# Splitting a layer norm into three pieces and joining two products in the third layer of a four-layer kernel

## The chip, the cores and the metric

One Trainium2 chip, one core. The metric is the device time of one execution in microseconds; the median of three runs is given. All tensors are float32.

## The reference, cut to what matters

Four layers work on `x` of shape (4, 128, 64, 64): four images, 128 channels, 4096 positions (tokens). Layer 0 is a state-space block between convolutions, layer 1 a 3x3 convolution, layer 2 a softmax attention with feed-forward and a mixture of experts, layer 3 a linear attention and a second mixture of experts. The change is about the norm before the attentions and about the linear attention:

```python
def _ln_t(v, eps=1e-5):
    m = jnp.mean(v, axis=-1, keepdims=True)
    s = jnp.var(v, axis=-1, keepdims=True)
    return (v - m) / jnp.sqrt(s + eps)
...
phi_q = jax.nn.elu(q) + 1.0
phi_k = jax.nn.elu(k) + 1.0
KV = jnp.einsum('blhd,blhm->bhdm', phi_k, v)
K_sum = phi_k.sum(axis=1)
Z = 1.0 / (jnp.einsum('blhd,bhd->blh', phi_q, K_sum) + EPS)
V_new = jnp.einsum('blhd,bhdm->blhm', phi_q, KV) * Z[..., None]
out = V_new.reshape(bs, seq, N_HEADS * HEAD_DIM) @ Wo + bo
...
t = t + _L3_attn_ref(_ln_t(t), ...)
```

There are 8 heads of 16 channels; `q`, `k` and `v` are affine images of the normed tokens. `Z` is one number per token and head, so it may be multiplied to `phi_q` instead of to the product with `KV`; and then `KV` (one 16x16 block per head, zero elsewhere) and `Wo` may be multiplied with each other once per image.

## The kernel before, in words

Channels lie on the 128 partitions, tokens along the free axis, in chunks of 512 columns (`CH`), eight to an image (`NCH`). [...]

The order of the work. The code is a Python program that is unrolled. A stage of a layer is a generator: `in_turn(n, *stages)` runs over rounds, and in round i it calls the stages from the last to the first, stage k on chunk i-k, with a `yield` after each. `run(*parts)` steps several generators in turn, one `yield` each (`in_turns`), and so fixes the order in which instructions are written. The tile framework then orders the instructions of each engine; an instruction that is ready may pass one that was written before it. Only the attention of the second layer, with its long score and exponential loops, has a fixed order for PE, DVE and POOL. A `psum.tile(..., tag="mm")` takes a bank from a pool of that tag (7 banks in the third layer, 8 in the second from the second image on, 4 for the first, 6 in the expert layers); the framework takes care that it is free.

The norm, `layernorm_steps` (from line 102). A product with `center` takes the mean off the chunk (`ln_xc`, L94); ACT squares it and copies it to `ln_kept` (L115, L116), and a `yield` follows. Four products with `mean` put the variances of 128 tokens each into 32 rows of `ln_var` (L94); DVE transposes 32x32 blocks (L122); the inverse root of 4 numbers per partition is made either by POOL's `pow` (L142, behind an addition of eps on DVE, L141; the third layer) or by a square root on ACT and a reciprocal on DVE (L127, L128; the second layer); four PE transposes of the broadcast root spread it over the channels, into the same PSUM tile `ln_var` (L131), and DVE multiplies it to `ln_kept` (L133; with gain and bias L135, L136).

Callers. In the second layer three places use it: `centred`/`norm` of `prepare` (32 chunks), `first_centred`/`first_norm` and `last_centred`/`last_norm` of `feed_forward` (32 chunks each), 96 norms in all. A first call runs to the `yield`, a second one, a stage later, runs the rest. `prepare` of image b+1 and `feed_forward` of image b run side by side between two attentions; the first `prepare` runs beside the end of the first two layers, the last `feed_forward` alone. In the third layer, `K.layernorm` runs the whole norm in one stage.

The third layer, `layer3_attention`. `summed(b)` has the stages `norm`, `keys` and `add` in `in_turn`: `keys` multiplies the normed chunk with the keys' and values' weights (`kv`), adds the bias (L2068), copies values (L2074) and makes the feature elu+1 (L2076 and L2045); `add` sums features times values into `kv_sum`, 129 columns wide, the last for the sum of the features. At its end `kvh` (the masked KV) and `ksh` (the masked K_sum) are made. `answered(b)` has the stages `queries` (q and its feature `e_q`), `weighed` (`den_ps` from `ksh`, `num_ps` from `kvh`; DVE transposes `den`, adds, inverts, transposes back to `z`, L2118 to L2123, and multiplies `z` with `num_ps` to `vn`, L2125) and `give` (product with `wo`, added to the image, L2131). `summed(0)` runs alone, then `summed(b+1)` beside `answered(b)`, then `answered(3)` alone.

The expert layers (`expert_ffn`) have a norm of their own, in which the spread goes into a tile of its own, `ln_rs` (L1865); the change doesn't touch them.

Of the kernel before, what the change touches and what calls it, by code (L numbers as in the profile page):

```python
# [9 lines left out]
F32 = mybir.dt.float32  # L10
# [3 lines left out]
ALU = mybir.AluOpType  # L14
# [3 lines left out]
P = 128  # L18
# [3 lines left out]
CH = 512  # L22
NCH = L // CH
# [7 lines left out]
class Common:  # L31
# [61 lines left out]
    def mm(self, out, lhsT, rhs, start=True, stop=True):  # L93
        self.nc.tensor.matmul(out, lhsT, rhs, start=start, stop=stop)  # L94
# [7 lines left out]
    def layernorm_steps(self, out, terms, work, psum, affine=None, bufs=2, more=None, power=False):  # L102

        nc = self.nc
        xc = psum.tile([P, CH], F32, name="ln_xc", tag="mm")
        for n, (lhsT, rhs) in enumerate(terms):
            self.mm(xc, lhsT, rhs, start=n == 0, stop=n == len(terms) - 1)
        shift, g, b = affine or (0.0, None, None)
        sq = work.tile([P, CH], F32, name="ln_sq", bufs=bufs)
        kept = work.tile([P, CH], F32, name="ln_kept", bufs=bufs)  # L110
        if more is not None:
            nc.vector.scalar_tensor_tensor(kept, xc, shift, more, ALU.add, ALU.add)
            nc.scalar.activation(sq, kept, AF.Square)
        else:
            nc.scalar.activation(sq, xc, AF.Square, bias=shift)  # L115
            nc.scalar.activation(kept, xc, AF.Identity, bias=shift)  # L116
        yield
        vp = psum.tile([P, CH], F32, name="ln_var", tag="mm")
        for k in range(4):
            self.mm(vp[32 * k : 32 * k + 32, 0:P], self.mean[:, 0:32], sq[:, P * k : P * k + P])  # L120
        vt = work.tile([P, 4, 32], F32, name="ln_vt")
        nc.vector.transpose(vt.rearrange("p a b -> p (a b)"), vp[:, 0:P])  # L122
        sd = work.tile([P, 4], F32, name="ln_sd")
        if power:
            self.inverse_root(sd, vt[:, :, 0])()
        else:
            nc.scalar.activation(sd.unsqueeze(2), vt[:, :, 0:1], AF.Sqrt, bias=self.eps5)  # L127
            nc.vector.reciprocal(sd, sd)  # L128
        by_block = vp.rearrange("p (g b i) -> p b g i", b=4, i=32)
        for k in range(4):  # L130
            nc.tensor.transpose(by_block[:, k], sd[:, k : k + 1].to_broadcast([P, P]), self.ident)  # L131
        if affine is None:
            nc.vector.tensor_tensor(out, kept, vp, ALU.mult)  # L133
        else:
            nc.vector.scalar_tensor_tensor(kept, kept, g, vp, ALU.mult, ALU.mult)  # L135
            nc.gpsimd.tensor_scalar(out, kept, b, None, ALU.add)  # L136

    def inverse_root(self, out, src):
# [966 lines left out]
def in_turn(n, *stages):  # L1105


    for i in range(n + len(stages) - 1):
        for k in reversed(range(len(stages))):
            if 0 <= i - k < n:  # L1110
                stages[k](i - k)
                yield


def in_turns(*parts):

    parts = list(parts)
    while parts:
        for p in list(parts):
            try:  # L1120
                next(p)
            except StopIteration:
                parts.remove(p)
                continue
            yield
# [13 lines left out]
def layer2_attention(K, xd, dpool, w, before, images):  # L1139

    nc, tc, mm = K.nc, K.tc, K.mm
# [4 lines left out]
    with ExitStack() as ctx:  # L1146
# [107 lines left out]
        def prepare(b, big, work, psum):  # L1254
# [3 lines left out]
            n = NTT * NH * (HD + 1)  # L1258
# [5 lines left out]
            heads, xs, nrms, laters, halves = {}, {}, {}, {}, {}  # L1264
# [8 lines left out]
                next(halves[c])  # L1273

            def norm(c):
                next(halves.pop(c), None)
                nc.sync.dma_start(out=nrm_d[b % 2][:, c * CH : (c + 1) * CH], in_=nrms[c])

            def products(c):
# [60 lines left out]
            stages = in_turn(NCH, fetch, centred, norm, products, running, store)  # L1340
# [258 lines left out]
        def feed_forward(b, dsum, work, psum, into=None):  # L1599
# [67 lines left out]
                next(halves[c])  # L1667

            def first_norm(c):
                next(halves.pop(c), None)  # L1670

            def cosines(c):
                zp = psum.tile([P, CH], F32, name="z_ps", tag="mm")
# [29 lines left out]
                next(lasts[c])  # L1703

            def last_norm(c):
                next(lasts.pop(c), None)
                o = sums.pop(c)
                x = loads[c]
                nc.gpsimd.tensor_tensor(x, x, o, ALU.add)
                if into is None:  # L1710
                    nc.sync.dma_start(out=xd[b][:, c * CH : (c + 1) * CH], in_=x)
# [300 lines left out]
def layer3_attention(K, xs, w):  # L2012
# [3 lines left out]
    with ExitStack() as ctx:  # L2016
# [32 lines left out]
        def summed(b):  # L2049

            nrm = big.tile([P, L], F32, name="nrm")
            kvp = pskv.tile([P, P + 1], F32, name="kv_sum")
            phis = {}

            def norm(c):
                cols = slice(c * CH, (c + 1) * CH)
                K.layernorm(nrm[:, cols], xs[b][:, cols], work, psum)

            def keys(c):

                k1 = work.tile([P, 4, P], F32, name="k1")
                v = vs[(b * NCH + c) % 3]
                for i in range(2):
                    kv = psum.tile([P, 2, 2 * P], F32, name="kv", tag="mm")
                    for j in range(2):
                        at = c * CH + (2 * i + j) * P
                        mm(kv[:, j, :], nrm[:, at : at + P], wkv)
# [12 lines left out]
            def add(c):  # L2080
                ph, v = phis.pop(c)
                for j in range(4):
                    t = 4 * c + j
                    mm(kvp, ph[:, j, :], v[:, j, :], start=t == 0, stop=t == NTT - 1)

            yield from in_turn(NCH, norm, keys, add)

            kss = work.tile([P, 1], F32, name="kss")
            nc.vector.tensor_copy(kss, kvp[:, P : P + 1])
            kvh = work.tile([P, P], F32, name="kvh")  # L2090
            nc.vector.scalar_tensor_tensor(kvh, bv, kss, kvp[:, 0:P], ALU.mult, ALU.add)
            nc.vector.tensor_tensor(kvh, kvh, K.same16, ALU.mult)
            ksh = work.tile([P, P], F32, name="ksh")
            nc.vector.tensor_scalar(ksh, K.same16, kss, None, ALU.mult)
            kept[b] = nrm, kvh, ksh

        def answered(b):
            nrm, kvh, ksh = kept.pop(b)
            phis, vns = {}, {}

            def queries(c):
                qp = psum.tile([P, CH], F32, name="q_ps", tag="mm")
                mm(qp, wq, nrm[:, c * CH : (c + 1) * CH])
                q1 = work.tile([P, CH], F32, name="q1")
                nc.scalar.activation(q1, qp, AF.Identity, bias=bq1)
                e = phis[c] = work.tile([P, CH], F32, name="e_q")
                nc.scalar.activation(e, qp, AF.Exp, bias=bq)
                feature(e, e, q1)

            def weighed(c):  # L2110

                ph = phis.pop(c)
                dp = psum.tile([P, CH], F32, name="den_ps", tag="mm")
                mm(dp, ksh, ph)
                np_ = psum.tile([P, CH], F32, name="num_ps", tag="mm")
                mm(np_, kvh, ph)
                dt = work.tile([P, CH // 32, 2, HD], F32, name="den_t")
                nc.vector.transpose(dt.rearrange("p a h d -> p (a h d)"), dp)  # L2118
                rd = work.tile([P, CH // 32, 2, 1], F32, name="rd")
                nc.vector.tensor_scalar(rd, dt[:, :, :, 0:1], 1e-5, None, ALU.add)  # L2120
                nc.vector.reciprocal(rd, rd)
                z = work.tile([P, CH // 32, 2, HD], F32, name="z")
                nc.vector.transpose(z, rd.to_broadcast([P, CH // 32, 2, HD]))  # L2123
                vn = vns[c] = work.tile([P, CH], F32, name="vn")
                nc.vector.tensor_tensor(vn, z.rearrange("p a h d -> p (a h d)"), np_, ALU.mult)  # L2125

            def give(c):
                op = psum.tile([P, CH], F32, name="o_ps", tag="mm")
                mm(op, wo, vns.pop(c))
                at = xs[b][:, c * CH : (c + 1) * CH]  # L2130
                nc.vector.scalar_tensor_tensor(at, op, bo, at, ALU.add, ALU.add)  # L2131

            return in_turn(NCH, queries, weighed, give)
# [85 lines left out]
```

## Time and profile before

| what | us |
|---|---|
| median of 3 runs | 9518.07 (9507.56 to 9523.9) |
| the profiled execution | 9513.52 |
| its span, first to last instruction | 9511.7 |
| PE busy in the span | 8601.4 (90%) |
| PE weight loads | 3291.5 (35%) |
| DVE busy | 7152.9 (75%) |
| ACT busy | 7275.5 (76%) |
| POOL busy | 4928.9 (52%) |
| mean granted TensorE clock | 0.934 of full |

How to read it: busy time is the union of an engine's instructions. PE is TensorE's matmuls, PEld its weight loads, which overlap the matmuls; a float32 product appears as two instructions of each. [...] work back to back is better read from start to start. "Idle before" in square brackets is the time in which the engine stood still before an instruction, with what ended it. L94 is the helper through which all products go, so they are told apart by their tiles. The attention of the second layer takes most of the span: four stretches of some 1290 us, in which PE and ACT are busy almost throughout.

### The profile page before, as it was taken

The numbers are of one execution on the slowest core, as the hardware profiler recorded it, in microseconds if no ns is written. First come the engines' busy times: TensorE is split into PE (matmuls) and PEld (weight loads), VectorE is DVE, ScalarE is ACT, GpSimd is POOL, SyncE is SP. The second block draws the span as 40 slices with busy tenths as digits, with TensorE's granted clock in tenths as the row PEclk, the third lists the DMA queues.
The fourth block names the chain that finished last, engine by engine and source line by source line (L and its number), as shares of the span: only waits on it lengthen the run. The fifth ranks groups of instructions, "written<-read, shape, count | busy, mean of one in ns | idle before, by whom it ended". The sixth has DMA issues, their size and how long they took to land.

```text
span 9511.7 us, 189086 instructions
## 1 busy us (share of the span) xinstructions
PE 8601.4 (90%) x74394; PEld 3291.5 (35%) x74394; DVE 7152.9 (75%) x7845; ACT 7275.5 (76%) x10493; POOL 4928.9 (52%) x3287
## 2 busy tenths in 40 slices
PE   5888888889879999979999979999979999998887
PEld 2222222234443333333333333333333333334444
DVE  2889898887858888868888867888876888863463
ACT  3766767654459999969999969999979999974232
POOL 1777687765535555545555545555555555542011
PEclk8888888889989999989999989999989999999998
DMA  4434435222221221141121132221132121132205
GB/s 121 118 86 115 103 87 121 66 67 82 84 72 40 40 40 40 30 120 37 39 39 39 38 100 51 40 40 40 40 85 58 40 40 40 40 100 66 70 10 169
DMA packets 580323, 631.22 MB, mean 66 GB/s; under 512 B 118816, under 2 KB 374888, under 8 KB 578536
## 3 DMA queue, kind: packets, MB, share of 16 engines
q1 hardware_dynamic: 579432, 619.12, 26.4%
q8 instruction: 586, 9.60, 0.4%
q14 instruction: 305, 2.50, 0.1%
HBM read 444.74 MB, written 106.97 MB: 58 GB/s over the span
## 4 chain that ended last, share of the span: by engine, by line
PE 60%; DVE 4%; POOL 2%; issue 2%; ACT 2%; DMA 2%; SPq 1%; DVEq 0%; POOLq 0%; ACTq 0%
PE ctx_ps L94 28%; PE acc_ps L94 14%; PE score L94 12%; PE ln_xc L94 1%; PE hid_ps L94 1%; DMA w<-in_L_ffn_weight 1%; PE kv L94 1%; PE ln_var L131 1%; POOL ln_sd L1856 1%; DVE ctx L1509 0%; SPq L1244 0%; PE pool L94 0%; DVE x L2009 0%; POOL q L1304 0%; ACT hid L1696 0%
## 5 line engine op out<-in xcount | busy, mean ns | idle before, releaser
L1575 ACT ACTIVATE ex<-score 128x1024 f32<-128x1024 f32 x5120 | 4927.2, 1039 | 220.7 <-PE score L94 134.6
L94 PE MATMUL ctx_ps<-ex,qt 128*32 128x512 f32 x20480 | 2734.0, 606 | 19.8 <-DVE ctx L1509 19.8
L1524 POOL TENSOR_TENSOR folded<-ex 128x1024 f32<-128x1024 f32 x512 | 1224.0, 2391 | 2102.6 <-ACT ex L1575 1837.4
L1581 DVE STREAM_TRANSPOSE turned<-ex 128x1024 f32<-128x1024 f32 x1536 | 1886.0, 1228 | 325.4 <-ACT ex L1575 325.1
L1557 DVE STREAM_TRANSPOSE turned<-ex 128x1024 f32<-128x1024 f32 x1532 | 1842.6, 1203 | 0.0
L94 PE MATMUL acc_ps<-turned,turned_v 128*32 128x256 f32 x24576 | 1769.3, 379 | 3.0 <-POOL qt L1262 2.3
L94 PE MATMUL score<-queries,keys 32*128 32x512 f32 x10240 | 1333.7, 497 | 39.1 <-POOL queries L1252 33.4
L937 DVE TENSOR_TENSOR_SCAN hs<-decay,carry,hs 128x512 f32<-128x512 f32 x1024 | 1242.6, 1265 | 104.7 <-ACT decay L933 92.6
L94 PEld LDWEIGHTS acc_ps<-turned,turned_v 128*32 128x32 f32 x24576 | 800.5, 110 | 1476.9 <-issue 1324.3
L941 POOL TENSOR_TENSOR hs<-hs,c_sb 128x1024 f32<-128x1024 f32 x512 | 1207.4, 2358 | 80.8 <-DMA c_sb<-c_d 40.8
L933 ACT ACTIVATE decay<-dt,a_neg 128x512 f32<-128x512 f32 x1024 | 692.7, 689 | 646.5 <-DVE hs L937 637.5
L94 PEld LDWEIGHTS score<-queries,keys 32*128 32x128 f32 x10240 | 512.4, 182 | 1133.3 <-ACT ex L1575 775.5
L1381 POOL TENSOR_TENSOR turned_v<-v,quarter 128x1024 f32<-128x1024 f32 x256 | 612.8, 2394 | 262.9 <-PE acc_ps L94 230.7
L1525 POOL TENSOR_TENSOR quarters<-folded 128x512 f32<-128x512 f32 x512 | 658.2, 1286 | 40.2
L94 PE MATMUL y_ps<-hs,pair 128*64 128x512 f32 x2048 | 642.7, 754 | 35.6 <-POOL hs L941 35.3
L926 DVE TENSOR_TENSOR hs<-dtx,b_ps 128x2048 f32<-128x2048 f32 x256 | 580.7, 2268 | 110.5 <-PE b_ps L94 47.7
L94 PEld LDWEIGHTS ctx_ps<-ex,qt 128*32 128x32 f32 x20480 | 406.1, 108 | 655.5 <-issue 599.4
L94 PE MATMUL b_ps<-dbc,state 32*64 32x512 f32 x1024 | 328.3, 722 | 181.3 <-DVE hs L926 181.1
L1575 ACT ACTIVATION_READ_ACCUMULATOR ex<-score 128x1 f32 x2048 | 439.8, 215 | 0.0
L940 POOL COPY carry<-hs 128x2 f32<-128x2 f32 x512 | 97.4, 190 | 641.9 <-DVE hs L937 605.7
L1509 DVE COPY ctx<-ctx_ps 128x512 f32<-128x512 f32 x256 | 176.9, 691 | 329.4 <-PE ctx_ps L94 325.5
L1566 DVE TENSOR_REDUCE dacc<-quarters 128x2 f32<-128x512 f32 x508 | 327.4, 644 | 0.0
(376 smaller groups left out, 8800.6 us busy)
## 6 DMA issues: line engine op xcount, KB each, us to landing
c_sb<-c_d SPq DMA_DIRECT2D x512, 128.0 KB
keys<-head_d SPq DMA_DIRECT2D x1024, 64.0 KB
queries<-head_d SPq DMA_DIRECT2D x1024, 64.0 KB
under<-image_d SPq DMA_DIRECT2D x192, 264.0 KB
dt<-dt SPq DMA_DIRECT2D x128, 256.0 KB
dtx<-dtx SPq DMA_DIRECT2D x128, 256.0 KB
v<-value_d SPq DMA_DIRECT2D x1024, 32.0 KB
w<-in_L_ffn_weight SPq DMA_DIRECT2D x32, 1024.0 KB
```

Of the source, the lines that this page charges most:

```text
L94: self.nc.tensor.matmul(out, lhsT, rhs, start=start, stop=stop)
L926: nc.vector.tensor_tensor(hs, dtx2, bb.unsqueeze(1).to_broadcast([P, NQ, CH]), ALU.mult)
L933: nc.scalar.activation(ex, dt2[:, q, :], AF.Exp, scale=a_neg[:, q, g : g + 1])
L937: nc.vector.tensor_tensor_scan(hs[:, q, :], decays[q - 2 * i], hs[:, q, :], carry[:, g, q : q + 1], ALU.mult, ALU.add)
L941: nc.gpsimd.tensor_tensor(hs[:, two, :], hs[:, two, :], cs.unsqueeze(1).to_broadcast([P, 2, CH]), ALU.mult)
L1381: nc.gpsimd.tensor_tensor(t, v.unsqueeze(2).to_broadcast([P, 4 * BT, 4, HD]), quarter.unsqueeze(1).to_broadcast([P, 4 * BT, 4, HD]), ALU.mult,
L1524: nc.gpsimd.tensor_tensor(hs, exs[:, :, 0], exs[:, :, 1], ALU.add)
L1525: nc.gpsimd.tensor_tensor(qs, hs[:, :, 0 : CH // 2], hs[:, :, CH // 2 :], ALU.add)
L1557: nc.vector.transpose(*upright)
L1566: nc.vector.tensor_reduce(at, qs, AX.X, ALU.add)
L1575: nc.scalar.activation(ex, sps[p], AF.Exp, scale=scale, accum_out=sums[:, t : t + 1] if summed else None)
L1581: nc.vector.transpose(*upright)
```

## The change

- `layernorm_steps` has a second `yield` behind the inverse root, and the spread goes into a new PSUM tile `ln_rs` (tag `mm`); `ln_var` is only 128 columns wide. `ln_kept` gets one buffer more, `ln_sd` four in place of two.
- In the second layer, the callers run the generator to its end, so there the two last pieces follow each other directly.
- In the third layer the norm is three stages: `centred`, `varied`, `norm`. A new `in_rounds` takes stages with their lags; in a round it calls `varied` of the chunk before, `add` of the third before, `keys` of the second before, `norm` of the chunk before and `centred` of its own, with a `yield` after each. `summed` so has five steps per chunk.
- At the end of `summed`, `kvh` is transposed and multiplied with `wo` to `kvo`.
- `weighed` leaves `num_ps` out and multiplies `z` to the features; `give` multiplies them with `kvo` in place of `wo`.

```diff
-        kept = work.tile([P, CH], F32, name="ln_kept", bufs=bufs)
+        kept = work.tile([P, CH], F32, name="ln_kept", bufs=bufs + 1)
...
-        vp = psum.tile([P, CH], F32, name="ln_var", tag="mm")
+        vp = psum.tile([P, P], F32, name="ln_var", tag="mm")
         for k in range(4):
-            self.mm(vp[32 * k : 32 * k + 32, 0:P], self.mean[:, 0:32], sq[:, P * k : P * k + P])
+            self.mm(vp[32 * k : 32 * k + 32], self.mean[:, 0:32], sq[:, P * k : P * k + P])
         vt = work.tile([P, 4, 32], F32, name="ln_vt")
-        nc.vector.transpose(vt.rearrange("p a b -> p (a b)"), vp[:, 0:P])
-        sd = work.tile([P, 4], F32, name="ln_sd")
+        nc.vector.transpose(vt.rearrange("p a b -> p (a b)"), vp)
+        sd = work.tile([P, 4], F32, name="ln_sd", bufs=4)
         if power:
             self.inverse_root(sd, vt[:, :, 0])()
         else:
             nc.scalar.activation(sd.unsqueeze(2), vt[:, :, 0:1], AF.Sqrt, bias=self.eps5)
             nc.vector.reciprocal(sd, sd)
-        by_block = vp.rearrange("p (g b i) -> p b g i", b=4, i=32)
+        yield
+        rp = psum.tile([P, CH], F32, name="ln_rs", tag="mm")
+        by_block = rp.rearrange("p (g b i) -> p b g i", b=4, i=32)
         for k in range(4):
             nc.tensor.transpose(by_block[:, k], sd[:, k : k + 1].to_broadcast([P, P]), self.ident)
         if affine is None:
-            nc.vector.tensor_tensor(out, kept, vp, ALU.mult)
+            nc.vector.tensor_tensor(out, kept, rp, ALU.mult)
         else:
-            nc.vector.scalar_tensor_tensor(kept, kept, g, vp, ALU.mult, ALU.mult)
+            nc.vector.scalar_tensor_tensor(kept, kept, g, rp, ALU.mult, ALU.mult)
...
+def in_rounds(n, *stages):
+    for i in range(n + max(lag for lag, _ in stages)):
+        for lag, stage in stages:
+            if 0 <= i - lag < n:
+                stage(i - lag)
+                yield
...
             def norm(c):
-                next(halves.pop(c), None)
+                for _ in halves.pop(c):
+                    pass
...
+            def centred(c):
+                cols = slice(c * CH, (c + 1) * CH)
+                halves[c] = K.layernorm_steps(
+                    nrm[:, cols], [(K.center, xs[b][:, cols])], work, psum, bufs=3, power=True
+                )
+                next(halves[c])
+
+            def varied(c):
+                next(halves[c])
+
             def norm(c):
-                cols = slice(c * CH, (c + 1) * CH)
-                K.layernorm(nrm[:, cols], xs[b][:, cols], work, psum)
+                next(halves.pop(c), None)
...
-            yield from in_turn(NCH, norm, keys, add)
+            yield from in_rounds(NCH, (1, varied), (3, add), (2, keys), (1, norm), (0, centred))
...
-            kept[b] = nrm, kvh, ksh
+            tp = psum.tile([P, P], F32, name="kv_t", tag="mm")
+            nc.tensor.transpose(tp, kvh, K.ident)
+            kvt = work.tile([P, P], F32, name="kvt")
+            nc.vector.tensor_copy(kvt, tp)
+            both = psum.tile([P, P], F32, name="kvo_ps", tag="mm")
+            mm(both, kvt, wo)
+            kvo = work.tile([P, P], F32, name="kvo")
+            nc.vector.tensor_copy(kvo, both)
+            kept[b] = nrm, kvo, ksh
...
-                np_ = psum.tile([P, CH], F32, name="num_ps", tag="mm")
-                mm(np_, kvh, ph)
...
-                nc.vector.tensor_tensor(vn, z.rearrange("p a h d -> p (a h d)"), np_, ALU.mult)
+                nc.vector.tensor_tensor(vn, z.rearrange("p a h d -> p (a h d)"), ph, ALU.mult)
...
-                mm(op, wo, vns.pop(c))
+                mm(op, kvo, vns.pop(c))
```

The drain shown for `norm` is made in the same way in `first_norm` and `last_norm` of the second layer.

More of the change, by code (lines that the diff above doesn't have):

```diff
@@ L1669, in first_norm @@
             def first_norm(c):
-                next(halves.pop(c), None)
+                for _ in halves.pop(c):
+                    pass
             def cosines(c):
@@ L1705, in last_norm @@
             def last_norm(c):
-                next(lasts.pop(c), None)
+                for _ in lasts.pop(c):
+                    pass
                 o = sums.pop(c)
@@ L2053, in summed @@
             phis = {}
+            halves = {}
+            def centred(c):
[6 more added lines that the diff above has]
+                next(halves[c])
             def norm(c):
-                cols = slice(c * CH, (c + 1) * CH)
-                K.layernorm(nrm[:, cols], xs[b][:, cols], work, psum)
+                next(halves.pop(c), None)
             def keys(c):
@@ L2094, in summed @@
             nc.vector.tensor_scalar(ksh, K.same16, kss, None, ALU.mult)
-            kept[b] = nrm, kvh, ksh
+            tp = psum.tile([P, P], F32, name="kv_t", tag="mm")
[7 more added lines that the diff above has]
+            kept[b] = nrm, kvo, ksh
         def answered(b):
-            nrm, kvh, ksh = kept.pop(b)
+            nrm, kvo, ksh = kept.pop(b)
             phis, vns = {}, {}
```

## The prediction

> **What bounds the kernel now.** I began with the page's 40 slices: between the four attention stretches and at the end lie short stages that the long ones hide. The rows of the tiles that the diff names gave their places, and one table of stretches their size. Its columns are length, busy time of PE, PE's weight loads, DVE, ACT, POOL, then TensorE's granted clock.
>
> ```profile
> 4057.00:4243.00 186.00, 134.07 (x608) 63.31 (x608) 108.36 (x232) 119.70 (x182) 92.89 (x108) 0.79 0.51 131
> 8487.00:8604.00 117.00, 98.89 (x437) 43.07 (x437) 49.25 (x107) 74.28 (x113) 56.35 (x44) 0.88 0.56 168
> 8872.00:8946.00 74.00, 49.32 (x250) 31.97 (x250) 23.33 (x55) 21.20 (x43) 8.06 (x8) 0.86 0.00 1
> 8946.00:9181.00 235.00, 203.10 (x908) 115.18 (x903) 157.18 (x327) 88.19 (x166) 24.16 (x24) 1.00 0.00 1
> 9181.00:9226.00 45.00, 32.21 (x66) 11.70 (x65) 32.70 (x56) 10.14 (x16) 0.00 (x0) 0.95 0.07 24
> ```
>
> The last three rows are the third layer: `summed(0)` alone, three joint blocks of 78.9 us (first key product to first key product: 8949.94, 9028.82, 9107.70), and `answered(3)` alone: 354 us. The first two rows are second-layer stages that call the same edited norm: preparing one image beside the feed-forward of another (three like this, 180 to 186 us), and the last feed-forward alone. The chain that ended last names PE in nearly every step of the joint blocks. One round on PE:
>
> ```profile
> 8972.37 1.02 PE L94 MATMUL ln_xc<-x,center 128*128 128x512 f32 x2
> 8973.23 0.83 PE L94 MATMUL kv_sum<-v,e_k 128*128 128x129 f32 x6
> 8974.08 0.43 PE L94 MATMUL ln_var<-ln_sq,mean 128*32 128x128 f32 x8
> 8974.43 1.13 PE L94 MATMUL q_ps<-nrm,wq 128*128 128x512 f32 x2
> 8975.40 0.39 PE L94 MATMUL kv_sum<-v,e_k 128*128 128x129 f32 x2
> 8975.62 1.02 PE L94 MATMUL o_ps<-vn,wo 128*128 128x512 f32 x2
> 8976.76 0.65 PE L131 MATMUL ln_var<-ident,ln_sd 128*128 128x128 f32 x4
> 8978.26 0.48 PE L94 MATMUL kv<-wkv,nrm 128*128 128x256 f32 x1 [0.85 <-DVE nrm L133]
> ```
>
> Start to start, a 512-column product costs 0.86 us. A round is 9.44 us: five such products (den, num, centring, q, o) 4.30, keys and values 1.72, kv_sum 0.86, means 0.35, spreading transposes 0.44, together 7.67; the other 1.8 us waits for the norm, inverse root first, then L133.
>
> These lines also show how the order is made. `q_ps` needs nothing of this round and its bank is free, yet six kv_sum instructions, later in the program, pass it; it runs straight behind `ln_var`, the tile asked for before it. So I read: a product that opens a new PSUM tile does not pass an older one of the same tag, while one that writes an open tile can be passed. L131 (into `ln_var`, already open) is passed by q and o. The expert layer has the other kind, a spread into a tile of its own:
>
> ```profile
> 8606.80 1.12 PE L94 MATMUL ln_xc<-x,center 128*128 128x512 f32 x2
> 8610.16 0.66 PE L1865 MATMUL ln_rs<-ident,ln_wide 128*128 128x128 f32 x4 [2.24 <-POOL ln_wide L1858]
> 8610.75 1.08 PE L94 MATMUL ln_var<-ln_sq,mean 128*32 128x128 f32 x16
> 8611.76 1.22 PE L94 MATMUL ln_xc<-x,center 128*128 128x512 f32 x1
> ```
>
> PE idles 2.24 us, though the next centring needs only x, there all along, and the next means' squares ended at 8608.56. Now a second-layer round:
>
> ```profile
> 8593.41 0.42 PE L94 MATMUL ln_var<-ln_sq,mean 128*32 128x128 f32 x8
> 8593.76 1.13 PE L94 MATMUL ln_xc<-x,center 128*128 128x512 f32 x2
> 8594.72 1.88 PE L94 MATMUL ln_xc<-hid,w2T 128*128 128x512 f32 x4
> 8597.86 0.65 PE L131 MATMUL ln_var<-ident,ln_sd 128*128 128x128 f32 x4 [1.26 <-DVE ln_sd L128]
> 8598.35 1.02 PE L94 MATMUL ln_xc<-hid,w2T 128*128 128x512 f32 x2
> ```
>
> From means to spread 4.0 us pass (a table load of 1.28, square root 0.30, reciprocal 0.18, handoffs); the next chunk's centring and part of its product fill 2.7 of them.
>
> **The change, part by part.** *Product with values gone* (`num_ps`): PE loses 0.86 us a chunk. In the 24 joint rounds that is on the path. In `answered(3)` it is not: there o waits for vn on DVE, 1.24 us in a 4.94 us round, with four products (3.44 us) on PE. `vn` reads features from SBUF where it read PSUM: e_q, both operands in SBUF, takes 686 ns, vn 687, so nothing.
>
> *Norm in three pieces, alone* (`summed(0)`): PE's work is 7.67-4x0.86=4.23 us a chunk, DVE's 2.70 (k 2x0.425, e_k 0.682, transpose 0.312, eps 0.170, L133 0.688). Now 7.82 us a warm round, 73 us in all. Means still follow their square closely (Square 0.60), though kv_sum can fill that; I take 4.8 a round, eight rounds 38, plus about 11 of fill (first chain to the first key product 6.25 today, one more round behind): 49, so -24. Bounds -15 and -28.
>
> *Joint blocks.* Without num PE has 6.8 us a chunk; DVE has 2.70 and for the answer 4.09 (e_q 0.686, den_t 0.717, two small 0.536, z 0.712, vn 0.687, x 0.750): 6.8 as well. But steps alternate one for one, and `summed` now has 40 steps against 24 in `answered` (24 and 24 before). So the answers end when 60% of the sums is done: DVE 8x4.09+0.6x21.6=45.7 us there, PE 40.9; behind it 40% of the sums alone, PE 13.5. Floor 59. `answered(3)` keeps DVE 83% busy (4.09 of 4.94): the first part 55, the tail 3.2 rounds of 5.0, 16; 71 against 78.9, so -8 a block, -24. Bounds -51 (blocks of 62) and 0.
>
> *Joined matrix*, once an image: a transpose, two 128x128 copies (nearest: the mask of kvh, 0.285 each), a product of 0.22, handoffs: about 1.7 us. It is needed only at `give(0)`, behind queries and den, so it lies beside them; I take +2 for four images, bounds 0 and +7. Extra buffers for `ln_kept` and `ln_sd` issue nothing.
>
> Third layer: -24-24+2 = -46 (bounds -75 and -13).
>
> *The second layer is edited too.* All callers use the same generator, and they run its rest in one go, so the order of tiles becomes mean, spread, next product. The spread now opens `ln_rs`, so by the reading above, z, centring, hid, rd and den products queue behind a spread that waits for its root, and ACT, DVE and POOL wait for them. Work is unchanged; cover is lost. In the last feed-forward (16 norms, means to spread 3.6 us on average, 8.1 us of it idle today) up to 48 us of products lose their place. Serially: PE's 99 plus 16x3 for the roots (about the shortest of today, once queues have drained), its other waits (12) taken to overlap: 147 against 117, +30; bounds +10 and +48. In a mixed stage 24 norms have 6.3 us between means and spread, PE idles 52 us, 32 of it for the root. Serially 134+24x3=206, +20; with the 20 us of other waits kept, 226, +40. I take +35, bounds +5 and +70. Three of them +105. The first preparation runs beside the convolution, whose products have another tag: +2. Second layer: +137 (bounds +25 and +260).
>
> Two rules of the Trainium skill bear on this. "Perfetto Trace Analysis", section "Optimization Strategy", says that consistent bubbles can mean that SBUF or PSUM doesn't suffice for the next tile. By it, a mean tile given back at its transpose, instead of after L133, helps or costs nothing: sum -46. The 2.24 us row speaks against it: of six banks at most four were in use. I go by the row. "TensorE: Matmul & The Clock Gate", section "Part 1: The HAM clock gate", halves the clock after an idle window of about 3.4 us: gaps of 3 us lie near it, and 0.79 and 0.88 above show stages already partly cold. If all 134 us of PE ran at 0.7 instead of 0.79, that is +17 a mixed stage; it is in the upper bound.
>
> **Sum.** 137-46=+91 us. The profiled execution took 9513.5 (span 9511.7 and 1.8 around it), so 9604.5; the median of the three runs, 9518.1, is 4.6 higher: 9609.
>
> **Rivals.** *Only the third layer moves.* If a waiting spread can be passed although it opens a tile, the second layer stays and -46 remains: 9472. For it: the idle in the expert layer could come from an order fixed with a shorter root in mind. Against it: q behind `ln_var`, and `summed(0)`, where PE idles 1.8 us a round with the next centring ready but asked for behind a waiting key product. The sign turns at 46 us, 0.48 us for each of the 96 second-layer norms. Chance 0.18.
> *The third layer doesn't get what it is promised.* DVE as second bound and the lone tail of `summed` leave -13 of -46, the second layer as forecast: 9518+137-13=9642. For it: the uneven steps; against it: 1.8 us idle in every round today. Chance 0.12.
> *The forecast*, +91: 0.70, its own range 9530 to 9690.
>
> **From these the numbers.** Measurement tells about 0.2% (19 us) from no change. Within it falls the forecast's low end (second layer near +50) and a sliver of the first rival: 0.07. Faster 0.17, slower 0.76. A range from 9480 to 9700 leaves out the better part of the first rival and the far end of the bounds, together 0.2.
>
> **What would show it.** Right: in the mixed and last second-layer stages PE waits for `ln_sd` grow from 32 and 8 us to 60 and more and 30 and more, products no longer stand between a `ln_var` and its `ln_rs`, the stages last 210 to 230 and about 147 us. In the third layer no `num_ps`, joint blocks near 71 us with a stretch that has sums only, `summed(0)` near 49. Wrong: second-layer stages within 5 us of today's, or a centring between means and spread. Attention and expert stretches keep their times.

## The result and the profile after

The changed kernel takes 9723.5 us (median of 4 runs, 9719.0 to 9727.4) against 9512.8 (4 runs, 9505.1 to 9523.9): a ratio of 1.022, 95% interval 1.0208 to 1.0232, so 211 us slower, where the prediction said 91 slower and at most 9700. The sign and its main cause hold, the size doesn't. The profiled execution took 9723.6 us, its span 9721.8. The stretches that answer to those shown of before, columns as there:

```profile
4057.00:4286.00 229.00, 125.17 (x573) 63.36 (x574) 106.92 (x225) 113.44 (x172) 88.19 (x104) 0.75 0.37 101
8665.00:8821.00 156.00, 102.76 (x431) 47.91 (x432) 50.80 (x105) 74.06 (x113) 56.51 (x44) 0.80 0.43 126
9092.00:9145.00 53.00, 40.71 (x240) 28.01 (x239) 22.28 (x53) 20.36 (x41) 8.06 (x8) 0.89 0.00 1
9145.00:9385.00 240.00, 195.87 (x873) 115.60 (x873) 156.30 (x332) 87.02 (x168) 24.65 (x24) 0.92 0.00 1
9385.00:9439.00 54.00, 34.54 (x54) 12.89 (x55) 33.05 (x61) 10.12 (x16) 0.00 (x0) 0.75 0.15 43
```

The first two rows are second-layer stages, their ends cut at round numbers. Over the whole first one PE is busy for 135.9 us, against 134.1 before, and yet the stage is far longer. Measured from the last product of one attention to the first score of the next, the mixed stages went from 190.6, 186.4 and 189.6 us to 248.4, 251.4 and 250.9 (+184), and the last feed-forward, up to `gate_ps`, from 118.4 to 158.2 (+40). The first preparation ends 4 us earlier, attention and expert stretches keep their times within 2 us. The second layer alone (184+40-4) explains the whole loss. The third layer takes 346.7 us instead of 353.5: -7 where -46 was forecast. In rows three to five, `summed(0)` fell from 73 to 53 us, but the joint blocks stayed (240 us together against 235) and `answered(3)`, from the last kv_sum on, grew from 47 to 54, at a clock of 0.75 instead of 0.95.

PE's waits in the last feed-forward (us in total, times, longest), after:

```profile
PE ln_rs L133 <- DVE ln_sd L128: 46.3, 16, 7.0
PE rd_ps L1669 <- POOL rc L1662: 3.6, 2, 2.0
PE den_t L1656 <- DMA den<-den_d: 3.3, 1, 3.3
```

It was 8.1 us in 8 waits. In the first mixed stage (one image's preparation beside another's feed-forward) the same wait is 104.2 us in 24 waits (before: 31.8 in 14): every norm waits now. PE's instructions in that last stage show why:

```profile
8767.92 0.43 PE L94 MATMUL ln_var<-ln_sq,mean 128*32 128x128 f32 x8
8772.10 1.12 PE L133 MATMUL ln_rs<-ident,ln_sd 128*128 128x128 f32 x4 [3.75 <-DVE ln_sd L128]
8773.01 1.92 PE L94 MATMUL ln_xc<-x,center 128*128 128x512 f32 x2
...
8780.64 0.43 PE L94 MATMUL ln_var<-ln_sq,mean 128*32 128x128 f32 x8
8783.64 0.62 PE L133 MATMUL ln_rs<-ident,ln_sd 128*128 128x128 f32 x4 [2.57 <-DVE ln_sd L128]
```

The spread follows its means with nothing between. Before, a centring and part of w2T stood there. The transposes behind the 3.75 us gap take 1.12 us instead of 0.62 and the next centring 1.92 instead of 1.13: the granted clock was 0.50 from 8772.0 to 8774.7, against 0.98 just before.

The order is fixed when the kernel is built. Products and transposes of PE between a norm's means and its spread, in the built order, the norms' own left out (the traces give the same counts):

| | mixed stage, 24 norms | last feed-forward, 16 norms |
|---|---|---|
| before | 173 | 70 |
| after | 0 | 0 |
| run 3, below | 176 | 72 |
| run 4, below | 391 | 177 |

### The profile page after: what moved, and what is told of

The parts are those of the page before. It is cut to its first block, busy times and chain, and to the rows that moved or that the text cites. A ratio compares the mean times of both kernels' runs of the same rounds, so it can differ in the third digit from the quotient of the medians.

```text
span 9721.8 us, 189019 instructions
## 1 busy us (share of the span) xinstructions
PE 8606.5 (89%) x74342; PEld 3312.1 (34%) x74342; DVE 7155.3 (74%) x7853; ACT 7268.6 (75%) x10487; POOL 4928.7 (51%) x3287
## 4 chain that ended last, share of the span: by engine, by line
PE 46%; DVE 4%; ACT 3%; POOL 2%; issue 1%; DMA 1%; SPq 0%; DVEq 0%; POOLq 0%; ACTq 0%
PE ctx_ps L94 20%; PE acc_ps L94 10%; PE score L94 9%; PE ln_xc L94 2%; DMA w<-in_L_ffn_weight 1%; PE ln_rs L133 1%; ACT hid L1709 1%; PE kv L94 1%; POOL ln_sd L1870 1%; PE hid_ps L94 0%; PE o_ps L94 0%; POOL q L1316 0%; PE pool L94 0%; DVE x L2023 0%; ACT L127 0%
## 5 line engine op out<-in xcount | busy, mean ns | idle before, releaser
L133 PE MATMUL ln_rs<-ident,ln_sd 128*128 128x128 f32 x512 | 110.9, 356 | 366.1 <-DVE ln_sd L128 364.3
```

## The experiments

The theories. **A, held order**: a spread that opens a tile of the products' tag keeps later products behind it, and that is the second layer's loss. Its rivals: **R1**, the other edits of the norm (buffers, 128-column means); **R2**, a shortage of PSUM banks. For the third layer: **B**, uneven steps (40 to 24) eat the gain; **C**, VectorE bounds the block; **G**, the joined matrix's chain stands ahead of the queries; **F**, PE idles more and its clock falls. Ratios are to the kernel before, with 95% intervals.

**1. One tile again, everywhere.** `ln_var` has 512 columns again and takes the spread.
```diff
...
-        rp = psum.tile([P, CH], F32, name="ln_rs", tag="mm")
+        rp = vp
```


> The changed kernel with one edit: the spread is written into the mean's tile again (ln_var with 512 columns), in all layers; the three pieces, the divided features, the joined matrix and the larger ln_kept and ln_sd stay. Theory A (held order: a spread that opens a tile of the products' tag keeps every later product behind it): the mixed stages return from about 250 us to 187 to 192, the last feed-forward from 158 to 118 to 120, PE's waits for ln_sd from 103 to about 32 us in a mixed stage; total 9500 to 9512, with the third layer's 7 us gain kept or a little less. Rival R1 (the other edits of the norm, its buffers and its 128-column means, cost the time): the mixed stages stay near 250 and the total near 9720.

Measured: 9505.2 us, ratio 0.9992 (0.9984 to 1.0001); mixed stages 185.2, 186.1, 183.2, last feed-forward 119.1, waits for `ln_sd` 35.7 us. The larger `ln_kept` and `ln_sd` are in this run, so they are not the cause; the 128-column means, which went back here, are judged by run 2. In the third layer the blocks became 85.2 and 83.4 us, against 79.3 and 78.6 with the own tile (run 6): there it is worth some 5 us a block.

**2. The own tile in the second layer alone, on the kernel before.**
```diff
+        rp = psum.tile([P, CH], F32, name="ln_rs", tag="mm") if apart else vp
```


> The kernel before with one edit: in the second layer's norms the spread opens a tile of its own (ln_rs, same tag as all products); buffers, third layer and joined matrix as before. Theory A: the whole loss and no gain, mixed stages 248 to 252, last feed-forward 157 to 160, third layer 353 to 354, total 9725 to 9740. R1 (buffers and means): mixed stages near 190, total near 9515.

Measured: 9733.0 us, ratio 1.0228 (1.0213 to 1.0243); stages 249.0, 248.2, 251.2 and 154.9, third layer 354.4. The means have 512 columns here and the buffers are those of before, so R1 falls: the new tile carries the whole loss; A holds.

**3. A tag of its own.**
```diff
+        rp = psum.tile([P, CH], F32, name="ln_rs", tag="rs", bufs=1) if apart else vp
...
-  bufs=8 if b > 0 else 4
+  bufs=7 if b > 0 else 3
```


> As the run with the second layer's own spread tile, but this tile has a tag and one bank of its own, and the other tiles keep seven of eight banks (three of four in the first preparation). Theory A (order is kept among tiles of one tag): products may pass the spread again, mixed stages 188 to 200, last feed-forward 117 to 125, total 9510 to 9545. Rival R2 (shortage of banks: a norm that holds a third bank keeps the next product's tile waiting): no better than with the shared tag, mixed stages 250 or more, total 9725 or more.

Measured: 9526.8 us, ratio 1.0015 (1.0008 to 1.0022). PE's waits for the root in the first mixed stage (103.6 us in run 2):

```profile
PE ln_rs L132 <- DVE ln_sd L128: 33.2, 14, 7.7
```

Stages 190.9, 190.8, 191.4 and 119.1: 7 us over those of before. (In this profile the third layer, which the edit doesn't touch, is 12 us longer too; see the last section.) The products have a bank less, and the loss is gone: R2 falls, and what holds the order is the shared tag. Run 4, which holds banks longer, agrees.

**4. Pieces apart in the second layer too.** `varied` steps stand between centring and norm at the three places of its lists of stages; the first:
```diff
+            def varied(c):
+                next(halves[c])
...
-            stages = in_turn(NCH, fetch, centred, norm, products, running, store)
+            stages = in_turn(NCH, fetch, centred, varied, norm, products, running, store)
```


> The changed kernel, and its second layer also places the three pieces of the norm apart: means and spread are two steps of each round instead of one, so that the spread's tile is asked for behind other products. Theory A (a product asked for before the spread may run before it): 16 products instead of none stand between means and spread, the waits for ln_sd fall below 30 us a mixed stage; mixed stages 180 to 195, last feed-forward 115 to 125, total 9480 to 9520. Rival R2 (shortage of banks): a norm that keeps its pieces open longer holds more, stages stay above 230, total above 9650. Against A as well: a longer way through the stages (two more steps) costs fill, some 10 us a stage.

Measured: 9447.5 us, ratio 0.9925 (0.9910 to 0.9939); mixed stages 168.7, 169.9, 168.2, below the forecast of either theory; last feed-forward 116.4. Waits for `ln_sd` at the spread, first mixed stage:

```profile
PE ln_rs L133 <- DVE ln_sd L128: 7.6, 3, 4.5
```

In the four stages together, the own tile that costs 224 us, asked for one step later, gains some 60.

**5. Pieces apart, but the mean's tile in the second layer.** Run 4's edit, and this one (`apart` is set by the third layer alone):
```diff
-    def layernorm_steps(self, out, terms, work, psum, affine=None, bufs=2, more=None, power=False):
+    def layernorm_steps(self, out, terms, work, psum, affine=None, bufs=2, more=None, power=False, apart=False):
...
-        rp = psum.tile([P, CH], F32, name="ln_rs", tag="mm")
+        rp = psum.tile([P, CH], F32, name="ln_rs", tag="mm") if apart else vp
```


> The run with the pieces of the norm apart in all layers (9447 us), but in the second layer the spread goes into the mean's tile; the third layer keeps its own spread tile. If only the place of the spread among the steps matters once the pieces are apart: mixed stages 166 to 172, last feed-forward 115 to 119, total 9440 to 9455. If the mean's tile, held over one more step of each round, now keeps products waiting for a bank: mixed stages 175 to 190, total 9465 to 9510.

Measured: 9466.1 us, ratio 0.9951 (0.9935 to 0.9968); mixed stages 175.8, 175.4, 175.1, last feed-forward 115.8. Run 1 has the same buffers and the mean's tile without the extra step, and mixed stages of 183 to 186. So the place of the spread gives some 10 us a stage, and the own tile, once apart, another 6 or 7. That is the low edge of the second expectation; whether its reason, a bank held longer, is the cause was not tried.

**6. The third layer's change alone** (second layer spreads into the mean's tile; the edit of run 5 on the changed kernel, without run 4's).


> The changed kernel with the second layer's spread written into the mean's tile as before; the third layer as changed (own spread tile, three pieces, joined matrix). Theory A: mixed stages 183 to 191, last feed-forward 119, third layer as in the changed kernel, 345 to 349; total 9498 to 9508, the third layer's net gain of some 7 us alone. Rival: if the forecast of -46 was right and only this one profile shows it small, total near 9470.

Measured: 9487.4 us, ratio 0.9973 (0.9962 to 0.9984): 26 us faster, between the two. In the profile the third layer is 343.8, some 10 us of the rest are shorter mixed stages (183.8, 186.2, 186.0). Other runs with larger `ln_kept` and `ln_sd` show the same, but run 8, with the buffers of before, has 187.7, 186.5 and 186.4; whether the buffers give 3 us a stage or chance does was not tried. This run is the base for 7, 9, 10 and 11.

**7. Pieces without the joined matrix** (`num_ps` and `wo` as before), on run 6.
```diff
-            tp = psum.tile([P, P], F32, name="kv_t", tag="mm")
...
-            nc.vector.tensor_copy(kvo, both)
...
+                np_ = psum.tile([P, CH], F32, name="num_ps", tag="mm")
+                mm(np_, kvh, ph)
...
-                mm(op, kvo, vns.pop(c))
+                mm(op, wo, vns.pop(c))
```


> The kernel before with only the third layer's norm in three pieces (own spread tile, 40 steps against 24), num_ps and its matrix kept. Theory B (uneven steps: the answers end early and the rest of the sums runs alone): summed(0) 50 to 56 instead of 73, but joint blocks 80 to 86, which gives the 20 us back: total 9500 to 9520. Rival D (the pieces as such shorten each round by the norm's wait of 1.8 us): joint blocks 66 to 70, total 9455 to 9475.

Measured: 9467.8 us, ratio 0.9952 (0.9939 to 0.9964); blocks 74.8 and 75.5, `answered(3)` 41.2, third layer 318.7. B missed, and D's total came true without its blocks (66 to 70). The joined matrix, which removes a product per chunk, makes the layer 25 us longer in the profiles, and the kernel 20 us by the medians.

**8. The joined matrix alone, on the kernel before.** The lines from `kv_t` to `kvo` and the product of `z` with the features come with it, as in the change.
```diff
-                np_ = psum.tile([P, CH], F32, name="num_ps", tag="mm")
-                mm(np_, kvh, ph)
...
-                mm(op, wo, vns.pop(c))
+                mm(op, kvo, vns.pop(c))
```


> The kernel before with divided features and joined matrix only; norm and order of steps (24 and 24) as before. Theory B (the product's 0.86 us is on the path in joint rounds, but each image's chain to the joined matrix now stands before its queries): -0.86 x 24 = -21, given back by 2 to 4 us for each of four images: third layer 340 to 346, total 9499 to 9505; joint blocks 74 to 76, answered(3) longer by 5 to 7. Rival C (answers are limited by VectorE's chain, so PE's shorter work buys nothing): joint blocks within 1 us of 78.9, total 9512 to 9520.

Measured: 9530.8 us, ratio 1.0020 (1.0013 to 1.0026): slower, blocks 81.2 and 82.9; both expectations missed. A round lasts 9.56 us with one product less, where it lasted 9.44. Part of one, all engines:

```profile
9071.31 0.61 PE L131 MATMUL ln_var<-ident,ln_sd 128*128 128x128 f32 x4
9071.34 0.69 DVE L2045 SCALAR_TENSOR_TENSOR e_q<-e_q,q 128x512 f32<-128x512 f32 x1 [1.27 <-ACT e_q L2115]
9071.95 0.74 DVE L2137 SCALAR_TENSOR_TENSOR x<-o_ps,bo,x 128x512 f32<-128x512 f32 x1
9072.61 0.68 DVE L133 TENSOR_TENSOR nrm<-ln_kept,ln_var 128x512 f32<-128x512 f32 x1
9073.34 1.99 PE L94 MATMUL kv<-wkv,nrm 128*128 128x256 f32 x8 [1.42 <-DVE nrm L133]
```

Before, DVE's order was x, nrm, e_q; here it is e_q, x, nrm. The norm's last step now waits behind two others after its spread, and keys wait 1.42 us instead of 0.85; the kv_sum ahead of the next means waits another 0.55 for `e_k`, whose chain num_ps had covered. That returns the product's 0.86 us and more.

**9. Five steps to three.**
```diff
+                sums, answers = summed(b + 1), answered(b)
+                for i in range(48):
+                    next(sums, None)
+                    if 3 * (i + 1) // 5 > 3 * i // 5:
+                        next(answers, None)
+                run(sums, answers)
```


> The run with the changed third layer and the old second layer, with one more edit: in the joint blocks five steps of the sums go with three of the answers, so that both end together. Theory B (uneven steps are what ate the gain): joint blocks 66 to 73 instead of 79 to 80, third layer 315 to 330, total 9470 to 9485. Rival C (VectorE's 6.8 us a chunk or the chain from den to o limits the block): blocks 76 to 80, total 9498 to 9508. Rival E (the serial start and end of each block, some 14 us at a low clock, are the larger part): blocks 74 to 77.

Measured: 9464.1 us, ratio 0.9952 (0.9938 to 0.9965); blocks 70.8 and 70.6, third layer 317.3. The block and layer lengths are B's. From the first key product of a block to its last kv_sum it is 55.2 us, where run 6 has 61 to 63, and the way on to the next key product is 1 to 2 us shorter: without num_ps the uneven steps cost 8 us a block. With num_ps kept, the same pace gives only 2 (run 12 against 7).

**10. The joined matrix made late.** The eight lines from `kv_t` to `kvo` move from the end of `summed` into `give`, run at c == 0 just ahead of its first product.
```diff
             def give(c):
+                if c == 0:
+                    tp = psum.tile([P, P], F32, name="kv_t", tag="mm")
...
+                    kvos.append(kvo)
                 op = psum.tile([P, CH], F32, name="o_ps", tag="mm")
-                mm(op, kvo, vns.pop(c))
+                mm(op, kvos[0], vns.pop(c))
```


> The run with the changed third layer and the old second layer (9487 us), with the transpose, the two copies and the product that make the joined matrix moved from the end of the sums to just ahead of the first o_ps of the answers. Theory G (the queries wait behind this chain): first q_ps about 3 to 6 us earlier in each of four images, from the last kv_sum to the first key product of the next image 11 to 12 instead of 15 us; third layer 325 to 335, total 9468 to 9480. Theory F (clock) alone: third layer within 5 us of 344, total 9482 to 9492.

Measured: 9462.3 us, ratio 0.9949 (0.9936 to 0.9961); blocks 72.4 and 72.7, `answered(3)` 43.7, third layer 315.6. The same work at another place takes 28 us off the layer, more than G had, and some 23 off the kernel by the medians. From the last kv_sum of an image to the next key product it is 11.0 us, where the base has 16 to 17; before that the blocks are as in the base. PE at the boundary of two images, first in the base (run 6), then here:

```profile
8987.58 1.16 PE L94 MATMUL kv_sum<-v,e_k 128*128 128x129 f32 x8 [2.32 <-DVE e_k L2059]
8989.77 0.33 PE L2121 MATMUL kv_t<-ident,kvh 128*128 128x128 f32 x1 [1.03 <-DVE kvh L2117]
8990.48 0.79 PE L94 MATMUL kvo_ps<-wo,kvt 128*128 128x128 f32 x2 [0.38 <-DVE kvt L2123]
8991.07 1.92 PE L94 MATMUL ln_xc<-x,center 128*128 128x512 f32 x2
8992.77 1.43 PE L94 MATMUL q_ps<-nrm,wq 128*128 128x512 f32 x2
...
8996.38 1.44 PE L94 MATMUL den_ps<-e_q,ksh 128*128 128x512 f32 x2 [1.82 <-DVE e_q L2059]
```
```profile
8975.64 1.02 PE L94 MATMUL q_ps<-nrm,wq 128*128 128x512 f32 x2
8977.02 0.41 PE L94 MATMUL ln_var<-ln_sq,mean 128*32 128x128 f32 x2 [0.36 <-ACT ln_sq L115]
8977.36 1.16 PE L94 MATMUL kv_sum<-v,e_k 128*128 128x129 f32 x8
8978.45 0.42 PE L94 MATMUL ln_var<-ln_sq,mean 128*32 128x128 f32 x6
8980.62 1.10 PE L94 MATMUL den_ps<-e_q,ksh 128*128 128x512 f32 x2 [1.75 <-DVE ln_sd L143]
```

In the base the first query and the next image's centring open their tiles after `kv_t` and `kvo_ps`, so they run behind the last kv_sum and behind DVE's `kvh` and `kvt`, and slowly (1.92 us, where 1.02 is usual; the granted clock of a later boundary was 0.73). Here they run ahead of the last kv_sum. It is mechanism A once more, in another place.

**11. A product that nothing reads**, in place of num_ps.
```diff
+                np_ = psum.tile([P, CH], F32, name="num_ps", tag="mm")
+                mm(np_, ksh, ph)
```


> The run with the changed third layer and the old second layer (9487 us), with a product put back where num_ps stood: the divisors' matrix by the features, written to a tile that nothing reads. It does no needed work. Theory F (without num_ps TensorE waits over 2 us in each round of the answers alone, and its clock falls to half, so products of 0.86 us take 1.9): answered(3) 44 to 48 instead of 54 at a clock of 0.9 or more instead of 0.75, the joint blocks unchanged to 3 us longer (0.86 us more work a chunk); total 9475 to 9490. Rival G (the joined matrix's chain and the queries behind it are the cost): answered(3) 52 to 55, blocks 80 to 86, total 9490 to 9510.

Measured: 9493.9 us, ratio 0.9979 (0.9972 to 0.9987); blocks 81.8 and 82.6, `answered(3)` 49.1: the blocks and the total are G's, the shorter answers nearly F's. That part for the base, this run and run 7, in this order:

```profile
9145.90:9200.00 54.10, 34.23 (x54) 12.49 (x54) 33.03 (x62) 10.13 (x16) 0.00 (x0) 0.75 0.16 43
```
```profile
9162.40:9211.50 49.10, 35.23 (x70) 12.85 (x70) 33.48 (x62) 10.11 (x16) 0.00 (x0) 0.88 0.14 35
```
```profile
9139.20:9181.00 41.80, 30.14 (x65) 11.63 (x66) 32.81 (x59) 8.86 (x14) 0.00 (x0) 0.98 0.08 26
```

With eight useless products the answers alone are 5 us shorter and the clock is 0.88 instead of 0.75. But this is one profile, and six others of this part, without num_ps and with the matrix made early, last 49.8 to 54.0 us at clocks of 0.73 to 0.84 (the changed kernel, runs 1, 4, 5, 8, 9). So F is likely there, not shown. In the blocks the product costs 3 us each, so F isn't the main cause. Run 10, without any such product but with the queries early, takes 43.7 us.

**12 to 14. Versions put together**: pieces apart in both layers and the five-to-three pace; 12 with num_ps kept, 13 as 12 but with the images as two streams without joint ends, 14 with the joined matrix made late. Their edits are those of runs 4, 7, 9 and 10 on the changed kernel; 13 has, in place of the pace by image (cut):
```diff
+        sums, given = one_by_one(*(summed(b) for b in range(1, NB))), answers()
+        for i in range(3 * 40):
+            next(sums, None)
+            if 3 * (i + 1) // 5 > 3 * i // 5:
+                next(given)
+        run(sums, given)
```

> A version put together from what the runs showed: three pieces of the norm placed apart in the second and third layers (spread in its own tile), num_ps and its matrix kept as before the change, and in joint blocks five steps of the sums to three of the answers. By the parts: second layer -65 as in the run with pieces everywhere, third layer -35 as in the run with the pieces only; the pace adds a further 3 x 4 to 3 x 8 where the lone tail was the loss (blocks 67 to 71) or nothing where PE's 7.67 us a chunk is the bound now (blocks 73 to 76). Total 9385 to 9415 by the first, 9410 to 9425 by the second.

Measured: 9415.0 us, ratio 0.9897 (0.9884 to 0.9911); blocks 73.1 and 73.2, third layer 315.6. The total and the blocks are those of the second expectation.

> The same version, but the images of the third layer follow each other without a joint end: the sums of image 1 to 3 are one stream, the answers another, five steps to three. If each block's serial start and end (11 us from the last kv_sum to the next key product) is loss that a stream hides: 8 us less for two of the boundaries, total 9370 to 9410 and 10 to 20 us below the paced one. If the next image's first norm can't start earlier since the answers' order holds it: equal to the paced one within 5 us.

Measured: 9416.7 us, ratio 0.9900 (0.9886 to 0.9913); blocks 73.1 and 73.2, third layer 314.3. From the last kv_sum to the next key product it is 12.9 us in both: the stream hides nothing of it.

> The changed kernel with three edits: pieces of the norm apart in the second layer too, the joined matrix made just ahead of the first o_ps, five steps of the sums to three of the answers. It stands beside the version that keeps num_ps and its matrix (9415 us, blocks of 73.2 us, third layer 315.6). If PE's time is what bounds an even block (forecast's step: 0.86 us a chunk on the path), blocks fall to 65 to 68 and the third layer to 290 to 302: total 9385 to 9402. If VectorE's chain from den to o bounds it (2 us of wait for vn a round in the answers alone): blocks 71 to 74, third layer 313 to 320, total 9408 to 9420.

Measured: 9414.2 us, ratio 0.9893 (0.9878 to 0.9908); blocks 70.3 and 71.9, third layer 314.8. The block isn't the 65 to 68 that was put down for PE as the bound. An even round, from key product to key product, in run 12 and then here:

```profile
8968.55:8977.31 8.76, 8.17 (x40) 4.85 (x38) 6.54 (x14) 3.71 (x7) 1.01 (x1) 1.00 0.00 0
8971.84:8979.75 7.91, 7.31 (x38) 4.47 (x36) 6.27 (x13) 3.72 (x7) 1.01 (x1) 1.00 0.00 0
```

PE has one wait in it, 0.6 us for `e_k`, and is busy for the rest. So in an even round num_ps's 0.86 us are on the path, and leaving it out gives 0.85. But a block has five such rounds, and its first one takes 10.4 or 12.0 us instead of 8.75, since `kv_t`, a wait of 1.6 us for `kvt`, `kvo_ps` and the first `o_ps` stand in it. That leaves 1 to 3 us a block. Nor do the gains of runs 9 and 10 add: 317.3 and 315.6 us apart, 314.8 together. All three versions beat both kernels, by 1.0% of the kernel before, and can't be told from each other.

## Why the prediction was right and wrong

The forecast was 91 us slower, and 211 were measured. Of the 120 us or so between, 83 lie in the second layer (137 forecast, 220 measured) and 39 in the third (-46 and -7).

- *The reading of the order* (a product that opens a new tile doesn't pass an older one of its tag): right, shown by runs 2 to 4 and the built order. The prediction's signs to look for came true (no product between `ln_var` and `ln_rs`, waits over 60 and 30 us), but not its lengths of the stages.
- *Second layer, +137*: right in kind, too small. The term "24x3 for the roots" failed: the 24 norms of a mixed stage wait 104 us, 4.3 each (16 wait 46 in the last feed-forward, 2.9 each, as the "16x3" had it). Of the 4.3 us, 2.0 are waits for DVE, ahead of the transpose and of the reciprocal (0.4 in the last feed-forward), mostly while it works on something else; the wait ahead of the root on ACT, table loads included, is the same in both, 1.5 and 1.6. The 3 us, which are not the shortest of before either (0.98), fit a stage with one image's work, and I took them for a stage with two. Putting 4.3 for 3 gives 134+104=238, and with the 8 us of other waits still there 246; measured 248 to 251. In the last feed-forward the "other waits taken to overlap" failed: some 9 us stay, and PE is busy 5 us longer at a lower clock (0.81 for 0.88): 103+46+9=158.
- *summed(0) alone, -24*: measured -20; a round takes 5.3 us where 4.8 was put.
- *num_ps on the path in joint rounds*: wrong for the order that was built, where PE waits for DVE in each round. Run 8 shows +0.1 us a round; in the uneven rounds of runs 6 and 7 (10.25 and 10.72 us, for one chunk of sums beside five thirds of an answer) leaving it out gives 0.5 us of 1.4. The wait for the norm, 1.8 us a round, is no idle share that stays when PE's work shrinks: in run 8 it grew. Where the rounds are even, the term is right (run 14: 0.85).
- *answered(3) unchanged*: wrong, +7: its queries start late (run 10), and the clock is 0.75 for 0.95; that PE's waits of some 2 us a round without num_ps do this is likely (run 11), not shown.
- *Joint blocks 71*: measured 79.4 and 79.8. From the first key product to the last kv_sum they take 61 to 63 us (70.3 before), from there to the next key product 16 to 18 (8.5 before): the growth at that boundary is what the forecast lacks. With the joined matrix made late they are 72.5. That this is near 71 is partly luck, for the parts differ: of the 6.4 us gained, the pieces alone bring 4 (run 7).
- *Joined matrix, +2, "lies beside queries and den"*: this is what failed in the third layer: its place costs 28 us in the profiles, some 23 by the medians (run 10). Its data are needed late, but its tiles are asked for ahead of the queries' tiles, and by the prediction's own reading of the order the queries then queue behind it. The rule was applied to the spread and not to `kv_t` and `kvo_ps`.
- *Bounds of the third layer, -75 and -13*: the terms' own bounds add to -79 and -8. The measured -7 lies outside both.
- *vn from SBUF: 0*: 681 ns on average, against 687; right.
- *The rules*: the Trainium skill, "Perfetto Trace Analysis", section "Optimization Strategy", says that consistent bubbles can mean that PSUM doesn't suffice for the next tile. Here it isn't so: in run 3, with a bank less for the products, PE waits 33 us for the roots of the first mixed stage, not 104. The clock rule ("TensorE: Matmul & The Clock Gate", section "Part 1: The HAM clock gate") agrees with the 0.50 behind the gap of 3.75 us, but the 17 us a mixed stage, put as an upper bound, didn't come: the clock of the first one fell from 0.79 to 0.75, and PE's busy time grew by 2 us.
- *Rivals*: that the third layer doesn't get what it is promised came true beside the forecast. The lone tail that it names is part of it (run 9); the late queries, which it doesn't name, account for 28 of the 39 us (run 10).

## What to carry to other kernels

Where tiles of one tag are handed out in program order, an operation that opens a tile and has to wait holds back every later product that opens one of that tag. Ask, for each new tile, what its first writer waits for and who asks next; count products between the two in the built order. A late step should write an open tile, have a tag of its own, or be asked for later in the program (against the kernel before, the same spread changed the four stages here by +224 us with the shared tag, +7 with a tag of its own, and -62 asked for later). Removing work from an engine gives its time only where that engine is busy round after round (0.85 of 0.86 us in run 14). Where each round waits for a chain across other engines it gave less or nothing, and in run 8 it cost, since the chain's order changed with it.

## What the runs showed of the hardware

- A product that nothing reads, eight times, came with a stretch of 49.1 us instead of 54.1 and a granted clock of 0.88 instead of 0.75 for TensorE (run 11); in six other profiles without it the stretch took 49.8 to 54.0.
- `summed(0)` in run 3 and in the kernel before has the same TensorE instructions in the same order, yet lasts 81.6 and 73.1 us, at clocks of 0.73 and 0.86. Whether that differs from execution to execution or between the two programs was not tried. So one profile's stretch of 70 us can't tell 8 us; where third-layer runs differ by less, only the medians count.
